# Two residual sums as identity products on TensorE, in a four-layer image kernel

## The chip, the core and the metric

The kernel runs on one core of a Trainium2 chip. The metric is the device time of one execution in microseconds (us). The kernel before was run three times: 5684.69, 5682.38 and 5680.2 us, a median of 5682.38 us.

A core has five engines with a queue of instructions each. PE (TensorE) multiplies matrices and writes only to PSUM, a small memory of eight banks; PEld is its weight load, which runs beside the products. DVE (VectorE), ACT (ScalarE) and POOL (GpSimd) work on tensors; SP only issues DMAs. Each queue is worked off in order, so an instruction that waits holds up all behind it on its engine.

## The reference

The input `x` has 16 images of 64 x 64 tokens (4096) with 256 channels, in float32. Four layers follow one another, each a group norm without scale, a function of it, and a residual sum:

```
x = x + nearest_code(gn(x))        # layer 0: nearest of 1024 code vectors, per token
x = x + attention_rows(gn(x))      # layer 1: sigmoid attention within each row of 64 tokens
x = x + gate(gn(x)) * gn(x)        # layer 2: a scalar gate per token, from a softmax over 4096
x = x + linear_attention(gn(x))    # layer 3: 4 heads of 32, output projection, layer norm over channels
```

In layer 1, `f`, `g` and `h` are projections of the normed input with biases; the scores of a row are `f g^T`, and `sigmoid(scores) h` is added to `x`. In layer 3 the output projection is normed over the channels, multiplied by `gamma`, and `beta` and the residual are added. Two residual sums are what the change touches: that of layer 1 and that of layer 3.

## The kernel before

**Layout.** An image is cut into 8 chunks (`NCHUNK`) of 512 tokens (`CW`). A chunk is mostly held channel-major, as a tile `[128, 2, 512]` of float32: partition is the channel within a half `k` of the 256 channels (`NK` = 2), the free axis is the token. Between stages the chunks go through DRAM (`x1_d`, `x2_d`, `x3_d`). The input is given twice, as tokens (`x`) and channel-major (`xT`); the output is written as tokens.

**Stages, per image.** `stats0` takes the first norm's statistics. `stage1` (layer 0) finds the codes: distances on PE (L403, 512 columns at a time, into a bank pair `pd`), the maximum on DVE (L409, L414), a gather by POOL (L415), transposes back to channel-major (L378, copied out by ACT at L381). `layer1` is described below. `rows2` and `stage2` (layer 2) form three rows per image and then 64 pairs of an exponential on ACT (L645) and a weighted sum on DVE (L648), each over 128 x 2048. `gate2` applies the gate (L702 on ACT, L703 on DVE). `stage3` (layer 3) makes a pass over the chunks for keys, queries and values (L765, L782), and then an output pass.

**Order.** Lines 932 to 968 plan the images: each stage of each image is a task with a start and a length in units of one image, and a heap merges the steps of all generators by their due times. So five or six stages of different images are interleaved in the queues of all engines. The order within each queue is fixed before the run; blocks marked `high_priority` are put ahead. In the middle of the run the pattern repeats for each image.

**PSUM.** `bank(...)` gives one bank of 512 float32 per partition, of four (`ps_m`). `wide(...)` gives a pair of banks, 1024 float32, of two (`ps_w`); the pairs are shared by `pd` (layer 0's distances), `ph` (layer 1's values) and `po` (layer 1's result).

**Layer 1's chunk.** `attend` projects the chunk `xt` (L482, L493), copies the values out (L502, ACT, 128 x 1024), forms the scores (L513) and the attention weights (L518, L522). `mix` multiplies: 8 products of 128 x 128 into the pair `po` (L533), DVE adds `po` to the chunk in place (L538, 128 x 1024), DVE takes the next norm's statistics of it (`bn_stats`, L266), and SP stores the chunk one step later (L545) and loads the chunk after next.

**Layer 3's output.** The chunk `xt` (L892 loads it again) is channel-major and the output is wanted as tokens, so for each pair of 128-token blocks PE transposes the residual into a bank (4 transposes of 128 x 128, L902), adds the projection with the query block as weights (2 products with 256 columns, L908) and adds a row vector over the channels by a product of a block of ones with `x_row` (L912, bfloat16). ACT copies the bank to `y` (L913), and SP writes 4 blocks of 128 tokens at a time (L923, L926), 256 channels of a token being contiguous.

`x_row` holds `xm_` = `beta` minus a mean, a vector over the channels. `put_row` (L145 to 158) makes it once per image, in the first chunk of the key pass (L789): `xm_` is copied on ACT, 8 idle bfloat16 products (`busy`, L135) run, the vector is turned by `by_identity` (L176), and it is split into three bfloat16 parts by two rounds of an ACT cast (L156) and a small product (L157), and a last cast (L158).

Two further lines serve the prediction as rows: L597, an ACT copy of a bank with a bias vector, and L381, an ACT copy after which DVE takes `bn_stats` of the copied chunk.

Of the kernel before, what the change touches and what calls it, by code (L numbers as in the profile page):

```python
# [16 lines left out]
P = 128  # L17
C = 256
# [25 lines left out]
def kernel(  # L44
# [25 lines left out]
    def bank(name):  # L70
        return ps_m.tile([P, 512], F32, tag="pm", name=name)
# [55 lines left out]
    def row_tile(name):  # L127
        t = const.tile([P, C], BF16, name=name)
        nc.gpsimd.memset(t, 0.0)
        return t  # L130
# [6 lines left out]
                skip_group_check=True,  # L137
            )

    h_row, qv_row, x_row = row_tile("h_row"), row_tile("qv_row"), row_tile("x_row")  # L140

    def twice(row):
        return row.unsqueeze(1).to_broadcast([P, 2, C])

    def put_row(dst, v, weight, tag, plus=None, idle=0):  # L145

        v3 = small.tile([P, NK, PARTS], F32, tag="v3", name=f"v3_{tag}")
        nc.scalar.copy(v3, v.unsqueeze(2).to_broadcast([P, NK, PARTS]))
        pb = bank(f"prow_{tag}")
        busy(pb, idle)  # L150
        row = pb[:PARTS, :C]
        weight(row, v3, plus)

        for n in range(PARTS - 1):
            top = small.tile([PARTS, C], BF16, tag="ptop", name=f"top_{tag}_{n}", bufs=1)
            nc.scalar.copy(top, row)  # L156
            nc.tensor.matmul(row, lhsT=below[:, n, :], rhs=top, start=False, stop=True, skip_group_check=True)  # L157
        nc.scalar.copy(dst[0:PARTS, :], row)  # L158

    def by_weight(w):  # L160
# [9 lines left out]
                    skip_group_check=True,  # L170
                )
        return make

    def by_identity(out, v3, plus):
        for k in range(NK):
            nc.tensor.matmul(  # L176
                out[:, k * P : (k + 1) * P], lhsT=v3[:, k, :], rhs=ident, start=(k == 0), stop=(k == NK - 1),
                skip_group_check=True,
            )


    e_raw = s2p.tile([P, NK, CODES], F32, tag="x0b", name="e_raw", bufs=2)
# [258 lines left out]
    def layer1(b):  # L441
# [84 lines left out]
        def mix(ch):  # L526

            at, h = ats.pop(ch), hs.pop(ch)
            po = wide(f"po_{tag}_{ch}")
            for k in range(NK):  # L530
                for t in range(CH):
                    m = (k * CH + t) * P
                    nc.tensor.matmul(  # L533
                        po[:, m : m + P], lhsT=h[:, t, k * P : (k + 1) * P], rhs=at[:, t, :, :].rearrange("p r i -> p (r i)"),
                        start=True, stop=True,
                    )
            X = xt[ch].rearrange("p k n -> p (k n)")
            nc.vector.tensor_tensor(X, po, X, ALU.add)  # L538
            chunk_stats(st2, xt[ch], ch)
            if ch + 2 < NCHUNK:  # L540
                load(ch + 2)
# [174 lines left out]

    def stage3(b):
        tag = f"s3_{b}"
        dst = out[b].rearrange("(t p) c -> p t c", p=P)
        x3 = x3_d.pop(b)  # L720
        scale, nmean, xm_ = norm3.pop(b)
        wk_n = wts.tile([P, NK, P], F32, tag="wk_n", name=f"wk_{tag}")
# [35 lines left out]
        for ch in range(NCHUNK):  # L758
            xt = xb.tile([P, NK, CW], F32, tag="xb", name=f"xk_{tag}_{ch}")
            nc.sync.dma_start(out=xt, in_=x3[ch])  # L760
            if ch > 0:
                normalize(ch - 1)
            pk = bank(f"pk_{tag}_{ch}")
            for k in range(NK):
                nc.tensor.matmul(pk, lhsT=wk_n[:, k, :], rhs=xt[:, k, :], start=(k == 0), stop=(k == NK - 1))  # L765

            now = nkm[:, ch : ch + 1]
            nc.vector.tensor_reduce(now, pk, AX.X, ALU.max, negate=True)
            if ch > 0:
                last = nkm[:, ch - 1 : ch]  # L770
                nc.vector.tensor_scalar(now, now, last, None, ALU.min)
                nc.scalar.activation(al[:, ch : ch + 1], last, AF.Exp, scale=-1.0, bias=now)
            kx = s3p.tile([P, CW], F32, tag="v2", name=f"kx_{tag}_{ch}", bufs=7)
            nc.scalar.activation(kx, pk, AF.Exp, bias=now, accum_out=ks[:, ch : ch + 1])
            qv = s3p.tile([P, CH, 2, P], F32, tag="u4", name=f"qv_{tag}_{ch}")
            qvs[ch] = qv
            for pr in range(CH // 2):
                pqv = bank(f"pqv_{tag}_{ch}_{pr}").rearrange("p (j n) -> p j n", j=2)
                for j in range(2):
                    t = 2 * pr + j  # L780
                    for k in range(NK):
                        nc.tensor.matmul(  # L782
                            pqv[:, j, :], lhsT=xt[:, k, t * P : (t + 1) * P], rhs=wqv_n[:, k, :],
                            start=(j == 0 and k == 0), stop=False, skip_group_check=True,
                        )
                nc.tensor.matmul(pqv, lhsT=ones3, rhs=twice(qv_row), start=False, stop=True, skip_group_check=True)
                nc.scalar.copy(qv[:, 2 * pr : 2 * pr + 2, :, :].rearrange("p j s n -> p j (s n)"), pqv)
            if ch == 0:
                put_row(x_row, xm_, by_identity, f"x_{tag}", idle=8)  # L789
            yield 5  # L790
            pkt = bank(f"pkt_{tag}_{ch}")
            for t in range(CH):
                nc.tensor.transpose(pkt[:, t * P : (t + 1) * P], kx[:, t * P : (t + 1) * P], ident)
            ek = s3p.tile([P, CH, P], F32, tag="v2", name=f"ek_{tag}_{ch}", bufs=7)
            nc.scalar.copy(ek.rearrange("p t d -> p (t d)"), pkt)
            if ch > 0:
                queries(ch - 1)

            q4 = qv[:, :, 0, :].rearrange("p t (h d) -> p t h d", d=DH)
            qm = small.tile([P, CH, HEADS], F32, tag="qm", name=f"qm_{tag}_{ch}")  # L800
            nc.vector.tensor_reduce(qm, q4, AX.X, ALU.max)  # L801
            nc.gpsimd.tensor_tensor(q4, q4, qm.unsqueeze(3).to_broadcast([P, CH, HEADS, DH]), ALU.subtract)  # L802
            nc.scalar.activation(qv[:, :, 0, :], qv[:, :, 0, :], AF.Exp)

            pc = bank(f"pc_{tag}_{ch}")
            for t in range(CH):
                nc.tensor.matmul(pc[:, :P], lhsT=ek[:, t, :], rhs=qv[:, t, 1, :], start=(t == 0), stop=(t == CH - 1))
            if ch > 0:
                nc.vector.scalar_tensor_tensor(
                    ctxa, ctxa, al[:, ch : ch + 1], pc[:, :P], op0=ALU.mult, op1=ALU.add  # L810
                )
            else:
                nc.vector.tensor_copy(ctxa, pc[:, :P])
            yield 5
# [75 lines left out]
        for ch in range(NCHUNK):  # L890
            xt = xb.tile([P, NK, CW], F32, tag="xb", name=f"xo_{tag}_{ch}")
            nc.sync.dma_start(out=xt, in_=x3[ch])  # L892
            qT = qs[ch]
            y = s3p.tile([P, CH, C], F32, tag="u4", name=f"y_{tag}_{ch}")
            for pr in range(2):
                if pr == 1 and ch + 1 < NCHUNK:
                    deviate(ch + 1)
                px = bank(f"pxo_{tag}_{ch}_{pr}").rearrange("p (j c) -> p j c", c=C)
                for j in range(2):
                    t = 2 * pr + j  # L900
                    for k in range(NK):
                        nc.tensor.matmul(  # L902
                            px[:, j, k * P : (k + 1) * P], lhsT=xt[:, k, t * P : (t + 1) * P], rhs=ident,
                            is_transpose=True, start=(j == 0 and k == 0), stop=False, skip_group_check=True,
                        )
                for j in range(2):
                    t = 2 * pr + j
                    nc.tensor.matmul(  # L908
                        px[:, j, :], lhsT=qT[:, t * P : (t + 1) * P], rhs=wctx[:, 1, :], start=False, stop=False,
                        skip_group_check=True,  # L910
                    )
                nc.tensor.matmul(px, lhsT=ones3, rhs=twice(x_row), start=False, stop=True, skip_group_check=True)  # L912
                nc.scalar.copy(y[:, 2 * pr : 2 * pr + 2, :], px)  # L913
                if pr == 0:
                    if ch + 2 < NCHUNK:
                        form(ch + 2)
                    if ch + 3 < NCHUNK:
                        fetch(ch + 3)
                else:
                    if ch + 2 < NCHUNK:  # L920
                        variance(ch + 2)
                    if before is not None:
                        nc.sync.dma_start(out=dst[:, (ch - 1) * CH : ch * CH, :], in_=before)  # L923
                yield 3
            before = y
        nc.sync.dma_start(out=dst[:, TOK // P - CH :, :], in_=before)  # L926

# [75 lines left out]
```

## Time and profile before

| | |
|---|---|
| median of three runs | 5682.38 us |
| the profiled execution | 5674.06 us |
| its span, first to last instruction | 5672.1 us |
| mean granted TensorE clock | 0.962 |
| DMA: moved, mean rate | 1059.26 MB, 187 GB/s |
| busiest DMA queue, share of 16 engines | 46.5% |

The profile is of one execution. Its page gives busy time and share for each engine, the chain of work that ended last, and groups of instructions: line, engine, operation, what is written from what, shape, count, busy time in total, mean of one in ns, and the idle time just before with what ended it. A float32 matrix product stands in the trace as two instructions, a transpose as one, a bfloat16 product as one. Matmuls are pipelined: a group's mean is one instruction's time from start to end, and the distance from start to start of the next, which the timeline shows, is what it takes from PE. The granted clock is the share of full speed that TensorE got in a stretch.

### The profile page before, as it was taken

How to read it: one execution, taken by the hardware profiler on the slowest of the kernel's cores; microseconds unless marked ns; L12 is line 12 of the kernel's file. 1: busy time of each engine (PE TensorE's matmuls, PEld its weight loads, DVE VectorE, ACT ScalarE, POOL GpSimd, SP SyncE). 2: the span in 40 equal slices, each digit the busy share in tenths (PEclk: the TensorE clock that was granted, in tenths of full speed). 3: DMA queues.
4: the chain of work that ended last, by engine and by line, in shares of the span. 5: the costliest groups of instructions: out<-in, count | busy, mean ns of one | idle time of the engine just before them, and what ended most of it. 6: DMA issues, size and time to landing. Idle time of an engine off the chain costs nothing.

```text
span 5672.1 us, 76096 instructions
## 1 busy us (share of the span) xinstructions
PE 5162.0 (91%) x26927; PEld 3189.6 (56%) x26927; DVE 5049.3 (89%) x7186; ACT 4571.1 (81%) x6642; POOL 1801.5 (32%) x1076
## 2 busy tenths in 40 slices
PE   7977889989999999999999999999999999987788
PEld 3534446545656566565655656565565656564556
DVE  7589799899999999999999999999999999988882
ACT  4468589888989898888978888898888879887873
POOL 2223234323333333334333333333333333321221
PEclk9988999999999999999999999999999999998889
DMA  8553744655665757566575656657575675745543
GB/s 254 174 178 84 232 115 144 214 163 185 196 198 175 224 159 236 171 211 198 185 234 155 216 185 200 210 173 236 160 224 183 201 219 156 222 149 176 200 157 119
DMA packets 521365, 1059.26 MB, mean 187 GB/s; under 512 B 52504, under 2 KB 266392, under 8 KB 512792
## 3 DMA queue, kind: packets, MB, share of 16 engines
q1 hardware_dynamic: 406288, 885.11, 46.5%
q0 software_dynamic: 73728, 67.14, 8.3%
q10 hardware_dynamic: 40968, 102.13, 4.6%
q8 instruction: 214, 3.51, 0.3%
q14 instruction: 167, 1.37, 0.1%
HBM read 751.18 MB, written 303.04 MB: 186 GB/s over the span
## 4 chain that ended last, share of the span: by engine, by line
PE 46%; DVE 17%; ACT 16%; issue 6%; DMA 5%; POOL 4%; SPq 0%; ACTq 0%; DVEq 0%; POOLq 0%
PE pd_s L403 14%; ACT ex_s L645 7%; DVE ex_s L648 7%; PE ph_l L493 4%; PE pxo_s L908 3%; PE pqv_s L782 3%; PE po_l L533 2%; PE pk_s L765 2%; ACT nn_s L398 2%; POOL qv_s L802 2%; PE pz_s L857 2%; DVE i_s L414 2%; DVE nn_s L409 2%; PE pxo_s L902 2%; PE pvr_s L865 2%
## 5 line engine op out<-in xcount | busy, mean ns | idle before, releaser
L648 DVE CUSTOM_DVE_ANT_0 ex_s<-ex_s,x2b 128x2048 f32<-128x2048 f32 x1024 | 2360.4, 2312 | 77.6 <-ACT ex_s L645 74.6
L645 ACT ACTIVATE ex_s<-x0b,nmax_s,x_r 128x2048 f32<-128x2048 f32 x1024 | 2138.6, 2089 | 40.7 <-DVE num_s L648 30.5
L403 PE MATMUL pd_s<-e,xn_s 128*128 128x512 f32 x4096 | 1971.1, 614 | 43.9 <-DVE m L409 27.9
L415 POOL DMA_INDIRECT xc_s<-in_emb_rows,i_s x512 | 1113.7, 2175 | 1852.7 <-DVE i_s L414 1337.5
L403 PEld LDWEIGHTS pd_s<-e,xn_s 128*128 128x128 f32 x4096 | 745.8, 195 | 778.8 <-issue 669.1
L409 DVE CUSTOM_DVE_ANT_0 nn_s<-pd_s,nn_s 128x1024 f32<-128x1024 f32 x512 | 619.9, 1212 | 113.5 <-PE pd_s L403 63.0
L414 DVE FIND_INDEX8 i_s<-m,nn_s 128x8 uint32<-128x1024 f32 x512 | 622.9, 1217 | 0.0
L398 ACT ACTIVATE nn_s<-ne,nx_s 128x1024 f32<-128x1024 f32 x512 | 582.5, 1143 | 33.1 <-DVE nx_s L369 18.7
L493 PE MATMUL ph_l<-wh_l,xt_l 128*128 128x256 f32 x2048 | 519.6, 390 | 28.7 <-DVE m L409 16.9
L782 PE MATMUL pqv_s<-wqv_s,xk_s 128*128 128x256 f32 x2048 | 489.3, 381 | 0.0
L493 PEld LDWEIGHTS ph_l<-wh_l,xt_l 128*128 128x128 f32 x2048 | 379.7, 192 | 138.9 <-issue 69.0
L782 PEld LDWEIGHTS pqv_s<-wqv_s,xk_s 128*128 128x128 f32 x2048 | 389.1, 191 | 120.6 <-issue 59.7
L802 POOL TENSOR_TENSOR qv_s<-qv_s,qm_s 128x512 f32<-128x512 f32 x128 | 221.6, 1731 | 662.6 <-DVE qm_s L801 363.2
L868 POOL TENSOR_TENSOR lrs_s<-lrs_s,mhalf 128x4 f32<-128x4 f32 x128 | 178.0, 1391 | 677.2 <-ACT lrs_s L867 663.3
L756 POOL TENSOR_TENSOR qv_s<-qv_s,qd_s 128x512 f32<-128x512 f32 x128 | 214.4, 1675 | 249.0 <-DVE qd_s L755 132.0
L533 PE MATMUL po_l<-blk,h_l 128*128 128x128 f32 x2048 | 282.1, 288 | 3.0 <-DVE m L409 1.5
L533 PEld LDWEIGHTS po_l<-blk,h_l 128*128 128x128 f32 x2048 | 260.6, 200 | 41.1 <-issue 24.5
L908 PE MATMUL pxo_s<-wctx_s,qo_s 128*128 128x256 f32 x1024 | 269.2, 386 | 2.2 <-DVE qo_s L876 2.2
L765 PE MATMUL pk_s<-xk_s,wk_s 128*128 128x512 f32 x512 | 256.0, 620 | 1.0 <-DMA xk_s<-x_g 0.9
L913 ACT COPY y_s<-pxo_s 128x512 f32<-128x512 f32 x256 | 147.5, 580 | 132.4 <-PE pxo_s L912 116.0
L378 PE MATMUL pt_s<-ident,xc_s 128*128 128x128 f32 x1024 | 156.7, 282 | 105.2 <-DMA xc_s<-in_emb_rows,i_s 79.0
L351 ACT ACTIVATE sq_s<-xt_s,first 128x512 f32<-128x512 f32 x256 | 200.2, 806 | 37.2 <-DMA x0b<-rows_r 21.0
(206 smaller groups left out, 7322.0 us busy)
## 6 DMA issues: line engine op xcount, KB each, us to landing
xs_s<-in_xT SPq DMA_DIRECT2D x128, 512.0 KB
xt_s<-in_xT SPq DMA_DIRECT2D x128, 512.0 KB
xc_s<-in_x SPq DMA_DIRECT2D x128, 512.0 KB
x_s<-xt_s ACTq DMA_DIRECT2D x128, 512.0 KB
xt_l<-x_s SPq DMA_DIRECT2D x128, 512.0 KB
x_l<-xt_l SPq DMA_DIRECT2D x128, 512.0 KB
xr_r<-x_l SPq DMA_DIRECT2D x128, 512.0 KB
xg_g<-x_l SPq DMA_DIRECT2D x128, 512.0 KB
```

Of the source, the lines that this page charges most:

```text
L398: nc.scalar.activation(nn, ne2, AF.Identity, bias=nx2[ch][:, t : t + 1])
L403: nc.tensor.matmul(pd[:, cols], lhsT=xn[ch][:, k, t * P : (t + 1) * P], rhs=e2[:, k, cols], start=(k == 0), stop=(k == NK - 1),)
L409: nc.vector.tensor_tensor_reduce(out=nn, in0=pd, in1=nn, scale=1.0, scalar=-3.0e38, op0=ALU.add, op1=ALU.max, accum_out=m8[:, 0:1],)
L414: nc.vector.max_index(i8, m8, nn)
L415: nc.gpsimd.indirect_dma_start(out=xc[ch][:, t, :], out_offset=None, in_=emb_rows, in_offset=bass.IndirectOffsetOnAxis(ap=i8[:, 0:1], axis=0),
L493: nc.tensor.matmul(ph[:, t, :], lhsT=X[:, k, t * P : (t + 1) * P], rhs=wh_n[:, k, :], start=(t % 2 == 0 and k == 0), stop=False, skip_grou ...
L533: nc.tensor.matmul(po[:, m : m + P], lhsT=h[:, t, k * P : (k + 1) * P], rhs=at[:, t, :, :].rearrange("p r i -> p (r i)"), start=True, stop ...
L645: nc.scalar.activation(ex, x0b, AF.Exp, bias=nmax[:, T : T + 1], scale=x01[:, T, 1:2], accum_out=den[:, h, T : T + 1])
L648: nc.vector.tensor_tensor_reduce(out=ex, in0=ex, in1=x2b, scale=1.0, scalar=0.0, op0=ALU.mult, op1=ALU.add, accum_out=num[:, h, T : T + 1],)
L765: nc.tensor.matmul(pk, lhsT=wk_n[:, k, :], rhs=xt[:, k, :], start=(k == 0), stop=(k == NK - 1))
L782: nc.tensor.matmul(pqv[:, j, :], lhsT=xt[:, k, t * P : (t + 1) * P], rhs=wqv_n[:, k, :], start=(j == 0 and k == 0), stop=False, skip_group ...
L908: nc.tensor.matmul(px[:, j, :], lhsT=qT[:, t * P : (t + 1) * P], rhs=wctx[:, 1, :], start=False, stop=False, skip_group_check=True,)
```

## The change

**Layer 1.** The residual comes in on PE: for each half `k`, a float32 product with `ident` as weights and the 512 columns of the chunk opens the bank, and the 4 products of L533 accumulate on it. DVE's sum is gone; ACT copies the pair of banks (128 x 1024) back into the chunk. The statistics stay on DVE.

**Layer 3.** The output is left channel-major. For each half `pr` of the channels, a float32 product of `ident` with the chunk's 512 columns opens a bank, and one product with a 128 x 128 block of the projection as weights and the 512 queries closes it. ACT's copy becomes an ACTIVATE that adds `xm_` as a bias vector, one value per partition. The transposes, the products with 256 columns, the product with `x_row`, and all that made `x_row` are gone. The DMA to the output writes 128 partitions with 4 KB contiguous each. The host reorders axes of the result.

```diff
-    h_row, qv_row, x_row = row_tile("h_row"), row_tile("qv_row"), row_tile("x_row")
+    h_row, qv_row = row_tile("h_row"), row_tile("qv_row")
...
-    def by_identity(out, v3, plus):
-        for k in range(NK):
-            nc.tensor.matmul(
-                out[:, k * P : (k + 1) * P], lhsT=v3[:, k, :], rhs=ident, start=(k == 0), stop=(k == NK - 1),
-                skip_group_check=True,
-            )
...
             po = wide(f"po_{tag}_{ch}")
             for k in range(NK):
+                nc.tensor.matmul(
+                    po[:, k * CW : (k + 1) * CW], lhsT=ident, rhs=xt[ch][:, k, :], start=True, stop=False,
+                    skip_group_check=True,
+                )
                 for t in range(CH):
                     m = (k * CH + t) * P
                     nc.tensor.matmul(
                         po[:, m : m + P], lhsT=h[:, t, k * P : (k + 1) * P], rhs=at[:, t, :, :].rearrange("p r i -> p (r i)"),
-                        start=True, stop=True,
+                        start=False, stop=(t == CH - 1), skip_group_check=True,
                     )
-            X = xt[ch].rearrange("p k n -> p (k n)")
-            nc.vector.tensor_tensor(X, po, X, ALU.add)
+            nc.scalar.copy(xt[ch].rearrange("p k n -> p (k n)"), po)
             chunk_stats(st2, xt[ch], ch)
...
-        dst = out[b].rearrange("(t p) c -> p t c", p=P)
+        dst = out[b].rearrange("c p (k n) -> c p k n", k=NK)
...
-            if ch == 0:
-                put_row(x_row, xm_, by_identity, f"x_{tag}", idle=8)
...
-            y = s3p.tile([P, CH, C], F32, tag="u4", name=f"y_{tag}_{ch}")
-            for pr in range(2):
+            y = s3p.tile([P, NK, CW], F32, tag="u4", name=f"y_{tag}_{ch}")
+            for pr in range(NK):
                 if pr == 1 and ch + 1 < NCHUNK:
                     deviate(ch + 1)
-                px = bank(f"pxo_{tag}_{ch}_{pr}").rearrange("p (j c) -> p j c", c=C)
-                for j in range(2):
-                    t = 2 * pr + j
-                    for k in range(NK):
-                        nc.tensor.matmul(
-                            px[:, j, k * P : (k + 1) * P], lhsT=xt[:, k, t * P : (t + 1) * P], rhs=ident,
-                            is_transpose=True, start=(j == 0 and k == 0), stop=False, skip_group_check=True,
-                        )
-                for j in range(2):
-                    t = 2 * pr + j
-                    nc.tensor.matmul(
-                        px[:, j, :], lhsT=qT[:, t * P : (t + 1) * P], rhs=wctx[:, 1, :], start=False, stop=False,
-                        skip_group_check=True,
-                    )
-                nc.tensor.matmul(px, lhsT=ones3, rhs=twice(x_row), start=False, stop=True, skip_group_check=True)
-                nc.scalar.copy(y[:, 2 * pr : 2 * pr + 2, :], px)
+                px = bank(f"pxo_{tag}_{ch}_{pr}")
+                nc.tensor.matmul(px, lhsT=ident, rhs=xt[:, pr, :], start=True, stop=False)
+                nc.tensor.matmul(px, lhsT=wctx[:, 1, pr * P : (pr + 1) * P], rhs=qT, start=False, stop=True)
+                nc.scalar.activation(y[:, pr, :], px, AF.Identity, bias=xm_[:, pr : pr + 1])
...
-                        nc.sync.dma_start(out=dst[:, (ch - 1) * CH : ch * CH, :], in_=before)
+                        nc.sync.dma_start(out=dst[ch - 1], in_=before)
...
-        nc.sync.dma_start(out=dst[:, TOK // P - CH :, :], in_=before)
+        nc.sync.dma_start(out=dst[NCHUNK - 1], in_=before)
...
-    o = nc.dram_tensor("out_0", (x.shape[0], TOK, C), F32, kind="ExternalOutput").ap()
+    o = nc.dram_tensor("out_0", (x.shape[0], NCHUNK, P, NK * CW), F32, kind="ExternalOutput").ap()
...
-    return r.results[0]["out_0"].reshape(x.shape)
+    y = r.results[0]["out_0"].reshape(x.shape[0], NCHUNK, P, NK, CW)
+    return y.transpose(0, 1, 4, 3, 2).reshape(x.shape)
```

## The prediction

> **What bounds the kernel now.** I read the page's engine line and its chain of the work that ended last first, since the change moves work from DVE to PE and ACT.
>
> ```profile
> PE 5162.0 (91%) x26927; PEld 3189.6 (56%) x26927; DVE 5049.3 (89%) x7186; ACT 4571.1 (81%) x6642; POOL 1801.5 (32%) x1076
> PE 46%; DVE 17%; ACT 16%; issue 6%; DMA 5%; POOL 4%; SPq 0%; ACTq 0%; DVEq 0%; POOLq 0%
> ```
>
> PE and DVE are equally busy, but the chain stands on PE for 46% of the span and on DVE for 17%. Busy shares are a mean over unlike stages, so I looked for the stretches. PE's wait for POOL's L756 recurs in the timeline at 2633.09 and at 2967.58 us: one image takes 334.5 us. I cut one image where the chain of waits changes its colour and asked for busy times of each engine in these five stretches (columns: stretch, length, busy us and instructions of PE, PEld, DVE, ACT, POOL, then the granted clock, DMA share, GB/s).
>
> ```profile
> 2633.00:2668.00 35.00, 33.92 (x165) 20.94 (x166) 31.71 (x52) 27.25 (x46) 13.62 (x11) 0.95 0.61 194
> 2668.00:2783.00 115.00, 107.02 (x578) 68.00 (x577) 106.31 (x151) 104.15 (x148) 39.46 (x20) 0.99 0.50 152
> 2783.00:2892.00 109.00, 105.93 (x641) 72.39 (x640) 102.12 (x140) 90.06 (x129) 32.80 (x18) 0.98 0.69 219
> 2892.00:2931.00 39.00, 33.69 (x165) 16.95 (x163) 38.29 (x52) 32.09 (x49) 15.75 (x11) 1.00 0.74 230
> 2931.00:2968.00 37.00, 34.22 (x146) 19.13 (x143) 34.39 (x56) 31.17 (x44) 15.10 (x7) 1.00 0.72 246
> ```
>
> I call them E, A, B, C and D. In B, a third of the image, PE is busy 97%, and the pieces of the chain there add up to 99.5 us on PE, 0.5 on ACT and none on DVE. Four pieces of it:
>
> ```profile
> 2823.07 0.86 PE pz_s L857 x2
> 2823.93 0.86 PE pd_s L403 x2
> 2824.79 0.86 PE pxo_s L908 x4
> 2827.12 1.98 PE po_l L533 x16
> ```
>
> Both edits sit here: by the same windows for single lines, B holds 64 of L533's 128 instructions per image (4 of 8 chunks of layer 1) and 56 of L908's 64 (7 of 8 chunks of layer 3's output). In A the chain is mixed: ACT 46.8 us, PE 33.0, DVE 17.9, POOL 8.5. In C it is 12.0 on DVE and 10.0 on PE; in D 14.2 on PE, 9.1 on DMA, 9.2 on DVE.
>
> **Prices on PE.** The PE timeline gives them from start to start:
>
> ```profile
> 2829.37 0.60 PE L902 MATMUL pxo_s<-ident,xo_s 128*128 128x128 f32 x4
> 2829.81 1.03 PE L908 MATMUL pxo_s<-wctx_s,qo_s 128*128 128x256 f32 x4
> 2830.67 0.38 PE L912 MATMUL pxo_s<-x_row,ones 128*128 128x512 bf16 x1
> 2830.89 0.95 PE L865 MATMUL pvr_s<-one,qz_s 128*128 128x1 f32 x8
> ...
> 2832.17 3.60 PE L403 MATMUL pd_s<-e,xn_s 128*128 128x512 f32 x8
> 2835.61 1.02 PE L857 MATMUL pz_s<-qo_s,gram_s 128*128 128x512 f32 x2
> ```
>
> Eight instructions of L403 are four float32 products with 512 columns: 2835.61 - 2832.17 = 3.44, so 0.86 us each. Half a chunk of layer 3's output costs 0.44 + 0.86 + 0.22 = 1.52 us.
>
> **Layer 1, per chunk.** PE gains two identity products, 2 x 0.86 = 1.72 us; 128 chunks make 220 us. An identity product that isn't a transpose has no cheaper row: L176, with `ident` as one operand, runs as two instructions too. DVE loses the add and ACT gains a copy of the same size out of a bank pair, for which L502 is the row:
>
> ```profile
> L538 DVE TENSOR_TENSOR xt_l<-po_l,xt_l 128x1024 f32<-128x1024 f32 x128 | 155.1, 1212 | 14.5 <-PE po_l L533 14.3
> L502 ACT COPY h_l<-ph_l 128x1024 f32<-128x1024 f32 x128 | 129.6, 1013 | 67.2 <-PE ph_l L498 64.9
> L913 ACT COPY y_s<-pxo_s 128x512 f32<-128x512 f32 x256 | 147.5, 580 | 132.4 <-PE pxo_s L912 116.0 <-issue 12.6 <-DMA out<-y_s 1.0
> L597 ACT ACTIVATE rows_r<-pr_r,brow_r 128x512 f32<-128x512 f32 x32 | 21.8, 682 | 55.3 <-PE pr_r L593 55.3
> ```
>
> So DVE -155 us and ACT +130 us. The first identity product waits for nothing new: its chunk is already read by L482 and L493, and the pair `po` has to be free as before. New is that DVE's `bn_stats` waits for ACT. Behind it on DVE stand L409, which frees a pair for PE, and L648. The same pattern exists at L381: there DVE waited 22.6 us in all for 256 statistics. And the copy stands on ACT in front of exponentials (2.09 us each) for which L648 waits; before, the add stood on DVE in the same way. A pair now comes free through ACT: PE waited 5.2 us for L502 at L403, a few us for L538. I take these waits as zero, with 0 to +23 us for the range; below zero is possible where DVE's own queue was the late one, at most the 14.5 us in L538's row.
>
> **Layer 3, per chunk.** Before 2 x 1.52 = 3.04 us of PE, after 4 products of 0.86 = 3.44: +0.40, times 128 is +51 us. ACT's copy gets a bias vector: L597 against L913, +0.10 us x 256 = +26 us; ACT has room in B (90 of 109, none of the chain). The output DMA keeps its place on SP; its issue takes 0.39 us against 0.32 for the channel-major store L545, and SP is nowhere on the chain, so zero, with the last DMA's few us as the most that could be won.
>
> **`x_row`, per image.** Gone are 8 idle products, L176 and two small products, 1.73 + 0.53 + 0.20 + 0.20 = 2.66 us in D's chain, 16 images 43 us of PE; ACT loses 3.1 + 11.2 + 5.7 = 20 us, off the path. Next late there is L756 on POOL (PE waits for it at 2967.58, 2 us idle), so the gain lies between 0 and 2.66; I take all, since the chain runs over these pieces and through L409 to that wait.
>
> **Sum.** PE +220 + 51 - 43 = +228 us, DVE -155, ACT +136. How much of it reaches the end differs by stretch; I weigh each engine's change by its share of the chain there over its busy time.
> - B: PE 4 x 1.72 + 7 x 0.40 = 9.7, times 99.5/105.9: +9.1. DVE and ACT: nothing on the chain; if PE's cover went, DVE would give back 3 adds, 3.6 us.
> - A: 3 chunks. PE 5.2 x 33/107 = +1.6; ACT 3.0 x 46.8/104 = +1.4; DVE -3.6 x 17.9/106 = -0.6. Together +2.4.
> - C: PE +0.6, ACT +0.4, DVE 2 adds -2.4 x 12/38 = -0.8: +0.2.
> - D: -2.7.
>
> That is +9.0 us per image of 334.5. The first image and the last two have no such B; there I take a third. 13 x 9.0 + 3 x 3.0 = +126 us. The whole span's shares are a second way: PE 228 x 0.46 x 5672/5162 = +115, DVE -155 x 0.17 x 5672/5049 = -30, ACT 136 x 0.16 x 5672/4571 = +27: +112. I take +118: 5674 + 118 = 5792 for an execution like the profiled one. That one lies 8 us under the median of the runs, so the forecast is **5800 us**, 2.1% slower.
>
> [...]
>
> **Rivals.**
> - *PE is the bound everywhere.* For it: PE is busy 94% in mid-run and the same wait always comes back to it. Then all 228 us at the clock of 0.98 count: 5682 + 233 = 5915. Against: in A the chain has 47 us on ACT and 18 on DVE, and PE has 8 us idle there.
> - *The idle time takes it up.* PE has 20.2 us idle in the cut image (335 less 314.8) and needs 228/16 = 14.3 more. With DVE's 9.7 us gone, PE's waits for DVE shrink: 5682. Against: the idle time lies in A, C and D, the load in B.
> - *Faster, because DVE sets the pace.* For it: DVE is busy 38.3 of 39 us in C, and 93% over the image. PE would have to come down to 1% idle: 314.3 us per period of 334.5 and 14.3 more, over 0.99, are 331.9 us, 2.6 less, 16 images -42: 5640. It decides from the point where PE's idle share falls under 1.8% (328.6 of 334.5); B, the densest stretch, still has 2.8%.
> - *The identity product is cheaper than an ordinary one* (one instruction as in a transpose, 0.43 us): PE +220 becomes +110 and +51 becomes -59, in all +8, DVE's -30 then decides, about 5675. L176 speaks against it.
>
> **Chances.** The forecast, between 5735 and 5880, has 0.68; PE as the bound everywhere 0.11; taken up 0.08; faster by DVE 0.11; cheaper product 0.02. A difference of under 0.2% is about what a measurement of this kernel can't tell from none. Faster by more 0.12, within 0.2% 0.08, slower by more 0.80. The range goes from the taken-up case to the edge of the forecast's own plus part of the first rival: 5680 to 5890. The unknown waits (-14 to +23) and the lost gain in D (+43) lie inside it.
>
> **What would show it.** L538 gone, a copy of about 1.01 us in its place; L533's line with two more float32 products of 0.86 us per chunk; layer 3's half chunk at 1.72 instead of 1.52 us; PE's busy time near 5390, DVE's near 4895, ACT's near 4705; the image's period at 342 to 344 us, the growth in the stretch where layer 3's output and layer 1 overlap; the chain with more PE and less DVE. Wrong if the period stays at 334 with PE over 98% busy, if the identity product starts its successor after 0.43 us, or if DVE's waits for ACT at L266 grow past 23 us.

## The result, and the profile after

The changed kernel takes 5724.57 us (median of four runs, 5719.19 to 5737.11), the kernel before 5681.29 us in four runs beside it: a ratio of 1.0079, interval 1.0061 to 1.0097. It is slower by 43 us, where 118 had been forecast: the right sign, and a third of the size. The profiled execution took 5722.29 us, its span is 5720.6 us, the mean granted clock 0.970.

The engine line and the chain of the changed kernel's page:

```profile
PE 5361.2 (94%) x25935; PEld 3125.8 (55%) x25935; DVE 4922.3 (86%) x7058; ACT 4689.3 (82%) x6706; POOL 1791.9 (31%) x1075
PE 63%; DVE 11%; ACT 9%; DMA 4%; issue 4%; POOL 3%; ACTq 0%; SPq 0%; POOLq 0%; DVEq 0%
```

PE is busy 199 us longer, but the span grew by 48.5. So PE's idle time fell from 510 to 359 us: three quarters of the added work went into it. In the groups (busy in total, mean ns of one, idle time before) the new operations have their expected prices. The line numbers of the changed kernel are lower by up to 20: L396 is the old L403, L644 the old L648, L530 the old L533.

```profile
L524 PE MATMUL po_l<-xt_l,ident 128*128 128x512 f32 x512 | 270.1, 609 | 1.5 <-DVE m L402 1.5
L534 ACT COPY xt_l<-po_l 128x1024 f32<-128x1024 f32 x128 | 128.7, 1006 | 52.2 <-PE po_l L530 51.5
L259 DVE BATCH_NORM_STATS2 st_l<-xt_l 128x6 f32<-128x512 f32 x256 | 163.9, 680 | 39.8 <-ACT xt_l L534 38.9
```

So has the new half chunk of layer 3, here in PE's timeline (start, duration): from start to start 0.86 us for the identity product and 0.86 for the projection, 1.72 in all.

```profile
2862.46 1.02 PE L893 MATMUL pxo_s<-xo_s,ident 128*128 128x512 f32 x2
2863.32 1.02 PE L894 MATMUL pxo_s<-qo_s,wctx_s 128*128 128x512 f32 x2
2864.18 1.02 PE L851 MATMUL pz_s<-qo_s,gram_s 128*128 128x512 f32 x2
```

Where the time came from shows in the starts of one instruction of each image, the product that brings the bias into layer 1's row (`prow_h_l<-ident,bh`), in both timelines. The table gives its start in us for some images and, in the last two columns, the mean distance of an image to the next (images are counted from 0):

| | image 1 | image 4 | image 8 | image 15 | end | images 4 to 6 | images 8 to 14 |
|---|---|---|---|---|---|---|---|
| before | 499.8 | 1353.1 | 2663.7 | 4999.6 | 5672.1 | 325.7 | 333.7 |
| after | 511.2 | 1377.5 | 2715.7 | 5055.0 | 5720.6 | 334.1 | 334.2 |
| difference | +11.4 | +24.4 | +52.0 | +55.4 | +48.5 | +8.4 | +0.5 |

**The loss lies in the first half of the images; the later half as a whole lost next to nothing.** What sets them apart: in the steady part of the run, images 6 to 13 also carry the input statistics of a later image on DVE, 16 operations of 680 ns each, 10.9 us per image. The row of the kernel before:

```profile
L266 DVE BATCH_NORM_STATS2 st_s<-xs_s 128x6 f32<-128x512 f32 x256 | 167.1, 680 | 12.3 <-DMA xs_s<-in_xT 12.0
```

The same starts tell it image by image. Before the change images 4 and 5, without these statistics, take 322.4 and 325.2 us, and images 7 to 13, with them, 332.1 to 339.0. After it, images 4 and 5 take 333.5 and 333.7 us, and images 7 to 13 take 333.6 to 335.9. So the change costs 11.1 and 8.5 us in images 4 and 5, and gains 0.8 in the mean of images 8 to 13. Image 14, which is late but carries no such statistics, pays 8.1 us again; it is the last but one and has some 13 us less on PE than the others, so it counts for less. (Image 6, in the table's column of early images, carries them already.)

One late image cut at the same three instructions in both kernels (products of `prow_h`, `pgr` and `prow_qv`; I call the stretches A, B and D; columns as in the prediction). Before:

```profile
2664.00:2782.00 118.00, 109.10 (x587) 68.57 (x585) 109.28 (x158) 106.61 (x153) 42.26 (x22) 0.99 0.49 147
2782.00:2924.00 142.00, 133.62 (x780) 88.02 (x779) 134.41 (x183) 117.56 (x169) 44.68 (x27) 0.99 0.69 219
2924.00:2998.00 74.00, 71.15 (x319) 40.10 (x317) 68.12 (x107) 60.05 (x94) 29.24 (x18) 0.98 0.72 235
```

After:

```profile
2716.00:2828.00 112.00, 110.74 (x594) 68.92 (x592) 108.12 (x157) 103.44 (x153) 36.19 (x22) 1.00 0.59 171
2828.00:2978.00 150.00, 149.34 (x737) 85.78 (x737) 141.36 (x189) 137.71 (x189) 50.01 (x30) 1.00 0.65 200
2978.00:3051.00 73.00, 68.08 (x292) 38.40 (x290) 55.52 (x94) 50.47 (x79) 26.56 (x17) 0.95 0.70 233
```

B grew by 8 us, as forecast, and A shrank by 6, which had not been. PE's idle time fell from 20.1 us to 6.8. DVE has 7 us more in B and 12.6 less in D though its work fell: the planner, which lays the queues by the steps' costs, laid another order. Counted in DVE's queue (cut where DVE scales the weights `wh` and `wqv`, L308, and at L834), the 64 pairs of exponentials of an image lie 22, 22 and 20 in A, B and D before, and 22, 27 and 15 after. In an earlier image the picture is simpler. Three images of each, before and after:

```profile
1353.00:2330.00 977.00, 937.42 (x5025) 583.55 (x5023) 922.91 (x1300) 852.06 (x1237) 339.97 (x195) 0.99 0.63 194
```

```profile
1377.00:2380.00 1003.00, 980.60 (x4837) 574.62 (x4835) 901.24 (x1277) 876.91 (x1249) 333.84 (x194) 0.99 0.61 189
```

PE goes from 96.0% to 97.8%; of 43 us more products (14 per image), 26 show in the time, and 17 found idle time here too. DVE, at 922.91 of 977 us, was busy 94.5% in these early images before the change, no less than in the late ones (93.4%). So it isn't shown that PE alone set their pace then.

### The profile page after: what moved, and what is told of

It is laid out like the page before. It is cut to its first block, busy times and chain, and to the rows that moved or that the text cites. A ratio compares the mean times of both kernels' runs of the same rounds, so it can differ in the third digit from the quotient of the medians.

```text
span 5720.6 us, 74037 instructions
## 1 busy us (share of the span) xinstructions
PE 5361.2 (94%) x25935; PEld 3125.8 (55%) x25935; DVE 4922.3 (86%) x7058; ACT 4689.3 (82%) x6706; POOL 1791.9 (31%) x1075
## 4 chain that ended last, share of the span: by engine, by line
PE 63%; DVE 11%; ACT 9%; DMA 4%; issue 4%; POOL 3%; ACTq 0%; SPq 0%; POOLq 0%; DVEq 0%
PE pd_s L396 21%; PE ph_l L486 6%; DVE ex_s L644 5%; PE pxo_s L893 4%; ACT ex_s L641 4%; PE pxo_s L894 4%; PE po_l L524 3%; PE po_l L530 3%; PE pqv_s L778 3%; PE pk_s L761 2%; PE pz_s L851 2%; DMA xc_s<-in_emb_rows,i_s 2%; PE pr_r L589 2%; PE pvr_s L859 2%; DVE i_s L407 2%
## 5 line engine op out<-in xcount | busy, mean ns | idle before, releaser
L644 DVE CUSTOM_DVE_ANT_0 ex_s<-ex_s,x2b 128x2048 f32<-128x2048 f32 x1024 | 2363.0, 2318 | 127.3 <-ACT ex_s L641 126.9
L396 PE MATMUL pd_s<-e,xn_s 128*128 128x512 f32 x4096 | 1960.7, 613 | 23.9 <-DVE m L402 16.1
L408 POOL DMA_INDIRECT xc_s<-in_emb_rows,i_s x512 | 1096.8, 2142 | 1996.1 <-DVE i_s L407 1594.8
L396 PEld LDWEIGHTS pd_s<-e,xn_s 128*128 128x128 f32 x4096 | 748.5, 195 | 786.4 <-issue 713.8
L486 PE MATMUL ph_l<-wh_l,xt_l 128*128 128x256 f32 x2048 | 507.7, 386 | 0.9 <-DVE m L402 0.9
L862 POOL TENSOR_TENSOR lrs_s<-lrs_s,mhalf 128x4 f32<-128x4 f32 x128 | 220.5, 1723 | 585.7 <-ACT lrs_s L861 565.2
L530 PEld LDWEIGHTS po_l<-blk,h_l 128*128 128x128 f32 x2048 | 271.0, 192 | 113.8 <-issue 111.6
L530 PE MATMUL po_l<-blk,h_l 128*128 128x128 f32 x2048 | 277.3, 276 | 0.0
L752 POOL TENSOR_TENSOR qv_s<-qv_s,qd_s 128x512 f32<-128x512 f32 x128 | 198.2, 1548 | 244.6 <-DVE qd_s L751 120.1
L893 PE MATMUL pxo_s<-xo_s,ident 128*128 128x512 f32 x512 | 272.7, 615 | 0.0
L524 PE MATMUL po_l<-xt_l,ident 128*128 128x512 f32 x512 | 270.1, 609 | 1.5 <-DVE m L402 1.5
L894 PE MATMUL pxo_s<-qo_s,wctx_s 128*128 128x512 f32 x512 | 267.1, 603 | 0.7 <-DVE qo_s L870 0.7
L895 ACT ACTIVATE y_s<-pxo_s,xm_g 128x512 f32<-128x512 f32 x256 | 174.3, 681 | 101.9 <-PE pxo_s L894 99.3
```

The lines of the kernel that those rows point to most:

```text
L396: nc.tensor.matmul(pd[:, cols], lhsT=xn[ch][:, k, t * P : (t + 1) * P], rhs=e2[:, k, cols], start=(k == 0), stop=(k == NK - 1),)
L408: nc.gpsimd.indirect_dma_start(out=xc[ch][:, t, :], out_offset=None, in_=emb_rows, in_offset=bass.IndirectOffsetOnAxis(ap=i8[:, 0:1], axis=0),
L486: nc.tensor.matmul(ph[:, t, :], lhsT=X[:, k, t * P : (t + 1) * P], rhs=wh_n[:, k, :], start=(t % 2 == 0 and k == 0), stop=False, skip_grou ...
L530: nc.tensor.matmul(po[:, m : m + P], lhsT=h[:, t, k * P : (k + 1) * P], rhs=at[:, t, :, :].rearrange("p r i -> p (r i)"), start=False, sto ...
L644: nc.vector.tensor_tensor_reduce(out=ex, in0=ex, in1=x2b, scale=1.0, scalar=0.0, op0=ALU.mult, op1=ALU.add, accum_out=num[:, h, T : T + 1],)
L893: nc.tensor.matmul(px, lhsT=ident, rhs=xt[:, pr, :], start=True, stop=False)
```

## The experiments

Theories: **the limits** (DVE's work sets the late images' pace before the change, PE's work the early ones', and PE's everywhere after it, so that a product costs nothing where DVE's add goes with it, and its time where PE was the limit); **the order** (waits that the queue order makes set the period, and each edit shuffles them); and, against both, **the prediction's even price** of 9 us in each image. All ratios are to the kernel before on the same chip, with their intervals; the last two columns are the mean distance of an image to the next in the profiled execution, which for layer 3 alone was the longest of four (5748.37 us), so that its distances are somewhat high.

| run | time, us | ratio | images 4 to 6 | images 8 to 14 |
|---|---|---|---|---|
| kernel before | 5675 to 5681 | 1 | 325.7 | 333.7 |
| changed kernel | 5724.57 | 1.0079 [1.0061, 1.0097] | 334.1 | 334.2 |
| layer 1 alone | 5738.84 | 1.0107 [1.0088, 1.0125] | 331.7 | 335.8 |
| layer 3 alone | 5726.23 | 1.0081 [1.0063, 1.0099] | 331.1 | 338.7 |
| products without use | 5705.93 | 1.0050 [1.0033, 1.0068] | 332.1 | 332.9 |
| copy without products | 5662.43 | 0.9975 [0.9961, 0.9989] | 335.0 | 329.2 |
| order held | 5803.50 | 1.0215 [1.0183, 1.0247] | 336.8 | 340.7 |
| before, fewer statistics | 5611.75 | 0.9880 [0.9854, 0.9906] | 326.2 | 325.6 |
| after, fewer statistics | 5714.22 | 1.0061 [1.0042, 1.0080] | 333.5 | 333.7 |
| layer 3 with its row | 5699.24 | 1.0026 [1.0011, 1.0042] | 328.6 | 334.1 |
| layer 1, late images | 5667.21 | 0.9983 [0.9966, 1.0000] | 326.2 | 333.1 |
| layer 1, early images | 5715.72 | 1.0068 [1.0041, 1.0096] | 331.5 | 333.1 |
| layer 1, late, half | 5657.40 | 0.9969 [0.9952, 0.9986] | 325.7 | 330.4 |
| after, with the row | 5770.28 | 1.0169 [1.0152, 1.0186] | 338.2 | 335.7 |

**The two edits by themselves.** Layer 1's edit alone, with layer 3 as before:

> Layer 1's edit alone; layer 3 and x_row as before. The busiest engine sets the period: PE needs 315 + 13.8 = 329 us per image, and at 98% busy that is 335 to 337 us, all images alike: about 5735 us, nearly the whole loss of the change. The forecast's theory (each stretch by its share of the chain): about +7 us per image, 5785 us.

Layer 3's edit alone, without `x_row`, with layer 1 as before:

> Layer 3's edit and the end of x_row alone; layer 1's add stays on DVE. Both theories: PE +3.2 and -2.7 us per image, DVE unchanged, so within 0.2% of before, 5670 to 5690 us. If the transposes or the row vector cost more than their rows say, under 5670.

The first came out at +63 us, near the lower figure, but not in all images alike (+6.0 us in the early ones, +2.1 in the late). The second, +51 us, was expected by neither theory. The two sum to +114, yet both together cost 43: the parts don't add, which no sum over single operations can give. What stands out in the layer-3 run is a wait in PE's list from 2700 to 4700 us (in total, times, longest) that takes 2.2 us in the kernel before:

```profile
PE pg_n L278 <- DVE mv_n L274: 20.9, 11, 4.4
```

**PE's load without DVE's relief, and the reverse.** The kernel before, in which each chunk's pair is first written by the identity products and then overwritten, so that DVE's add stays:

```diff
             for k in range(NK):
+                nc.tensor.matmul(
+                    po[:, k * CW : (k + 1) * CW], lhsT=ident, rhs=xt[ch][:, k, :], start=True, stop=True,
+                    skip_group_check=True,
+                )
                 for t in range(CH):
```

> The kernel before with two identity products more per chunk of layer 1, whose result is thrown away: the next products clear the bank. PE +220 us, DVE and ACT unchanged. If PE's idle time takes the products up whatever DVE does: about as layer 1's edit alone, 5735 us. If DVE's relief paid for most of them: 5780 us or more.

And the kernel before with ACT's copy in place of DVE's add and no products; layer 1's residual is left out of the computation:

```diff
-            X = xt[ch].rearrange("p k n -> p (k n)")
-            nc.vector.tensor_tensor(X, po, X, ALU.add)
+            nc.scalar.copy(xt[ch].rearrange("p k n -> p (k n)"), po)
```

> The kernel before with layer 1's residual left out: ACT copies the bank pair into the chunk, DVE adds nothing, PE has no products more. DVE -155, ACT +130, PE unchanged. If DVE set the pace in the images that also take statistics of a later image (periods of 334 to 339 us): 5 to 9 us less in each of them, 5615 to 5645 us. If PE set the pace throughout: within 0.2% of before.

163 us more of PE cost only 30, less than any theory said: 6 us in an early image, nothing in a late one. DVE's relief gained 13 us, less than expected, since it gained 4 to 5 us in a late image and lost 9 in an early one. The early loss isn't PE's work, which is as before; PE's list of waits from 1375 to 2380 us, three images, begins with one that the kernel before hasn't among its first:

```profile
PE pgt_s L665 <- DVE gate_s L662: 19.5, 3, 6.8
```

This is a wait of another order, and the first sign that both theories hold a part.

**The order by itself.** The changed kernel, in which the last 14 exponential pairs of an image's second row may not stand ahead of the last query scale of the image before in DVE's queue. No operation is added. The pairs then lie 21, 22 and 21 over the three stretches: nearly as before the change (22, 22 and 20), but with one more in D.

```diff
+            mark = [i for i in nc.cur_bb.bb.instructions if i.engine == sums[0, 0, 0].ins.engine][-1]
+            for T in range(18, NT):
+                if (b + 1, 1, T) in sums and b + 1 < nb - 1:
+                    tc.add_manual_dep(
+                        sums[b + 1, 1, T].ins, mark.name,
+                        mybir.DependencyInfo(mybir.DependencyClass.NoSync, mybir.DependencyReason.DATA), reason="hold",
+                    )
```

> The changed kernel with one thing added: the exponential sums (b+1,1,18) to (b+1,1,31) may not stand ahead of image b's query scale in VectorE's queue, so that a late image's pairs of exponentials lie 22/22/21 over the three stretches as in the kernel before, and not 22/27/15. No operation is added or taken away. Theory 1 (the planner paid for the identity products by moving five pairs into the dense stretch; the order carries the gain): the late images' period goes from 335 us to 341 to 342, 10 of them, and the time to 5780 to 5800 us, a ratio of 1.018 to 1.021. Theory 2 (the idle time of TensorE takes up the products whatever the order): 5715 to 5735 us, 1.007 to 1.010, period 334 to 336.

It came out at 1.0215, a period of 340.7: the order carries 6 us per late image. The same three stretches, to be laid beside those of the changed kernel:

```profile
2730.10:2843.10 113.00, 111.63 (x601) 70.17 (x600) 104.44 (x153) 104.66 (x151) 42.65 (x21) 1.00 0.55 168
2843.10:2987.10 144.00, 142.93 (x706) 80.91 (x704) 125.63 (x174) 124.49 (x175) 42.51 (x27) 0.99 0.63 198
2987.10:3071.70 84.60, 74.10 (x317) 41.01 (x318) 73.41 (x113) 62.95 (x94) 30.85 (x19) 0.96 0.68 220
```

PE is busy 328.7 us as against 328.2: the work is the same. Its idle time is 12.9 instead of 6.8. B is 6 us shorter and D 11.6 longer. In D's timeline, one image later, PE stands idle for the statistics that DVE makes behind two exponential sums:

```profile
3394.13 1.88 PE L396 MATMUL pd_s<-e,xn_s 128*128 128x512 f32 x4
3400.03 0.56 PE L278 MATMUL pg_n<-mv_n,dmat 128*128 128x2 f32 x2 [4.02 <-DVE mv_n L274]
...
3403.04 1.91 PE L396 MATMUL pd_s<-e,xn_s 128*128 128x512 f32 x2
```

The wait is that of the layer-3 run. In the changed kernel the same `pg_n` starts without one. From 2700 to 4700 us it takes 22.9 us in six waits here, 3.8 per image, so that with the slower clock behind such a wait (0.50 behind one of them, last section) it may make up most of the 6 us.

One count fits this wait in every profile. The two runs that hold 21 pairs in D, this one and layer 3 alone, have it (22.9 and 20.9 us); all other kernels hold 15 to 20 there and have 0 to 2.9 us of it, or 8.2 without layer 1's residual. So the 6 us may be the price of that one pair more, and not of the five that the changed kernel had moved; this run doesn't separate the two.

**DVE's work by itself, before and after.** For the eight images from the ninth on, DVE copies 8 columns of a chunk in place of the input's statistics, and those images are normed with the figures of an earlier image. This edit in the kernel before:

```diff
-            chunk_stats(st, xt, ch)
+            if b <= EARLY:
+                chunk_stats(st, xt, ch)
+            else:
+                nc.vector.tensor_copy(seen, xt[:, 0, 0:8])
...
+        if b > EARLY:
+            norm0[b] = tuple(first[:, b - EARLY - 1, n, :] for n in range(3))
+            return
```

> The kernel before with the statistics of the input left out for the images past the first eight (VectorE copies 8 columns of a chunk in place of four bn_stats, and those images are normed by the figures of an image that was read earlier), which takes some 10.9 us of VectorE's 314 off a late image. Theory 1 (VectorE's 314 us of 335 set the pace of the late images before the change): period 324 to 328, some 60 to 80 us less, 5600 to 5620 us, a ratio of 0.987 to 0.990. Theory 2 (waits between the engines in their order set it, no engine alone): period 331 to 335, 5640 to 5680 us, 0.994 to 1.000.

The same edit in the changed kernel:

> The changed kernel with the same statistics left out. Theory 1 (TensorE sets the pace now, and VectorE has time to spare): period stays at 333 to 335, 5705 to 5725 us, a ratio of 1.005 to 1.009. Theory 2 (waits between the engines set it, VectorE still among them): period 328 to 331, 5655 to 5685 us, 0.997 to 1.002.

Their engine lines, in this order:

```profile
PE 5127.8 (91%) x26839; PEld 3165.9 (56%) x26839; DVE 4988.4 (89%) x7106; ACT 4566.7 (81%) x6618; POOL 1799.4 (32%) x1060
```

```profile
PE 5347.7 (93%) x25847; PEld 3110.4 (54%) x25847; DVE 4884.8 (85%) x6978; ACT 4687.8 (82%) x6682; POOL 1777.6 (31%) x1059
```

Before, 61 us less of DVE took 70 us off the time. (The statistics left out are the 10.9 us per image of the expectation, though two per chunk and not four; the small copies put in their place took 3.4 back.) But the edit also leaves out 11 small instructions per image on PE, those that finish the norm, and PE was busy 34 us less. So each microsecond of DVE was worth a little over one (70/61) if PE's part counted for nothing, as the limits theory has it, and 0.6 if it counted in full. The copy without products gave less: in a late image 4.5 us for 9.3 of DVE, 0.5 for each. After, 38 us less of DVE and 13.5 less of PE took off some 10, and the intervals of the two ratios overlap. The same instructions went in both kernels, so the difference between 70 and 10 isn't PE's small products: the limit of the late images has changed its engine. Both times and both periods lie in the bands of the limits theory.

**Layer 3 with its row.** Layer 3's edit alone, with `put_row(x_row, ...)` kept at its place and read by nothing:

> The edit of layer 3 alone, with the row of the residual's mean still built at the first chunk of the key pass (its eight idle products and six small ones too) and used by nothing. Against the run of the layer-3 edit alone (1.008), theory 1 (what cost time there was that this row's products no longer stand in a stretch where TensorE waits, and the products behind them run at the lower clock or late): 5675 to 5690 us, a ratio of 1.000 to 1.003. Theory 2 (the last pass in its new form costs it, by 51 us of products and 400 of ScalarE's copies at another shape): 5725 to 5755 us, 1.008 to 1.014.

1.0026 for 1.0081: with 14 instructions *more* on PE per image (43 us in all by the forecast's prices) this kernel is faster. The ratio is in the first theory's band, the time 9 us above it. The wait for `mv_n` is back at 2.2 us. Without the row's steps the planner had put 21 pairs in D and 21 in A, with them 20 and 22: one pair less ahead of the statistics that PE waits for.

**Where layer 1's products cost.** Layer 1's edit, for some images and chunks alone, layer 3 as before. The condition is `b >= EARLY` (from the eighth image), `b < EARLY` (the first seven), and `b >= EARLY and ch % 2 == 0`:

```diff
+            onpe = b >= EARLY
             for k in range(NK):
+                if onpe:
+                    nc.tensor.matmul(
+                        po[:, k * CW : (k + 1) * CW], lhsT=ident, rhs=xt[ch][:, k, :], start=True, stop=False,
...
+            if onpe:
+                nc.scalar.copy(X, po)
+            else:
+                nc.vector.tensor_tensor(X, po, X, ALU.add)
```

> Layer 1's edit alone and only in the images from the eighth on, whose stretches carry the statistics of a later input on VectorE; the first seven keep the add of VectorE. Theory 1 (two limits: VectorE sets the pace of the late images before the change and TensorE of the early ones, so the products cost some 10 us in each early image and nothing in a late one): 5665 to 5700 us, a ratio of 0.998 to 1.004, late period 333 to 337. Theory 2 (each image pays about the same, 8 to 9 us, as the prediction had it): 5735 to 5760 us, 1.010 to 1.014.

> Layer 1's edit alone and only in the first seven images. Theory 1 (two limits): the whole loss of the layer-1 edit alone (1.0107) is here: 5725 to 5755 us, a ratio of 1.008 to 1.013, with the periods of the fourth to eighth image 331 to 336 and the late ones as before. Theory 2 (each image pays about the same): about half of it, 5700 to 5715 us, 1.004 to 1.006.

> Layer 1's edit alone, in the images from the eighth on, and there in the chunks 0, 2, 4 and 6 only: a late image has 8.5 us more on TensorE (315 to 324) and 6 less on VectorE (314 to 308). Theory 1 (two limits): both engines stay under 97 % of a shorter period, 327 to 331 us: 5610 to 5660 us, a ratio of 0.988 to 0.996. Theory 2 (each image pays for its products): 5705 to 5720 us, 1.004 to 1.007. Theory 3 (the order that the planner lays sets the period, by several us either way): no number; anything beyond 1.002 or between the two would speak for it.

In the late images the edit costs nothing: 93 us more of PE, 79 less of DVE, and 12 us off the time, at the edge of what can be told from none. In the early ones it costs 36 us of the whole edit's 63 (1.0068 of 1.0107). That is between the two theories' bands, and its interval, 1.0041 to 1.0096, reaches into both: the mark of image 8 stands 53 us later than before, and the late images give some of it back, while with the edit in all images they lose 15 us more. The even price fails in the first run; the second can't decide. The half edit has the lowest time of the versions that compute the reference (0.9969), ahead of both kernels; its interval overlaps with that of the late images alone. It lies at the weak edge of what the limits would give: its period is 330.4 where 327 to 331 was expected, its time 5657 us where 5610 to 5660 was, its ratio just above 0.988 to 0.996.

The third theory keeps a part here too: a late image has the same instructions in the run of layer 1 alone and in that of the late images alone, and its period, over the five images 9 to 13, is 336.7 in the one and 330.3 in the other.

**The row beside both edits.** The changed kernel, with the row built again and read by nothing:

> The changed kernel with the row of the residual's mean built again at the first chunk of the key pass (eight idle products and the small ones, some 43 us of TensorE in all, 2.7 per image) and used by nothing. Theory 1 (TensorE sets the pace of the changed kernel in every image, so each product more is paid): 5745 to 5770 us, a ratio of 1.012 to 1.017. Theory 2 (the row's products help by themselves, as they did beside the layer-3 edit alone, 1.0026 with the row for 1.0081 without): 5690 to 5710 us, 1.002 to 1.006.

```profile
PE 5394.7 (94%) x26159; PEld 3129.3 (54%) x26159; DVE 4935.7 (86%) x7058; ACT 4704.5 (82%) x6770; POOL 1773.5 (31%) x1076
```

33 us more of PE's busy time made it some 46 us slower (51 by the ratios, 40 by the profiled spans). The same steps that helped beside the layer-3 edit alone are paid in full here, 20 us by image 8 and 11 more in the next seven. After the change, PE's microseconds are the ones that count. That 33 us cost more than themselves isn't explained; the order may have its part in it.

## Why the prediction was right in sign and wrong in size

**The prices held.** An identity product took 0.86 us, the copy out of the bank pair 1.006 us (from L502: 1.013), the copy with a bias 681 ns (from L597: 682), layer 3's half chunk 1.72 us. Busy time changed by +199 us on PE (forecast +228), -127 on DVE (-155), +118 on ACT (+136). On PE, a part of the difference is that untouched products ran shorter (L533's mean fell from 288 to 276 ns, at a mean clock of 0.970 for 0.962).

**The step that failed is the sum: "That is +9.0 us per image of 334.5", taken 13 times.** It priced a microsecond of each engine by that engine's share of the chain in one late image, and carried the price to all images. Two things are wrong in it.

- *The price of DVE in a late image.* "DVE -3.6 x 17.9/106 = -0.6" in A, and nothing in B. The two runs that took work from DVE before the change put its price in a late image between 0.5 and a little over one, not at 0.2. A share of the chain says what ended last, not what the time would do if that engine had less work: in these late images taking work from DVE shortened the period, though the chain passed mostly through PE and ACT. In the cut of the result, B came out as forecast (+8 for the +9.3 of B and C), D at -1 for -2.7, and A at -6 for +2.4. So the late images paid 0.5 us each for the forecast 9.0.
- *One image for all.* The image cut was a late one. In images 4 to 6, where DVE has less to do, the price was 8.4 us. That it is near the forecast's 9.0 is luck: the forecast worked its figure out for a late image, and here PE went from 96.0% to 97.8% busy.

Of the span's 48.5 us, 11.4 are there by image 1, 40.6 come between images 1 and 8, 3.4 between 8 and 15, and the end gives 6.9 back.

**The rivals.** "The idle time takes it up" is what happened in the late images, and its mechanism is the one named: PE's waits for others shrank, from 20.1 us to 6.8 (20.2 less 14.3 had been worked out). The argument against it, "the idle time lies in A, C and D, the load in B", failed because the change doesn't leave the queue order as it was: five pairs of exponentials moved from D to B, and A became 6 us shorter. That this move is what made the idle time usable isn't shown: where the pairs were held back the period was 6 us longer, but D then held one pair more than before the change, too. "DVE sets the pace" had the mechanism of the late images before the change; that it gained nothing agrees with the rival's own condition, that PE's idle share has to fall under 1.8% for a gain: after the change it is 2.0%. "PE is the bound everywhere" is now true of the kernel after, not of the one before.

**The waits.** DVE's wait for ACT's copy was given 0 to 23 us. It is 38.9, outside that range; 27.9 of it lie in the first 500 us, where the add waited 8.0 before. The mark of image 1 is 11.4 us late, and these 20 us of wait may be a part of that; no run separates it. From 2700 to 4700 us the wait doesn't occur.

**PE's busy share.** In the changed kernel the products are busy 98.0% of a late image, and 33 us more of products cost 46: there the busy share of a late image showed what set its pace. Before the change, at 94% in a late image, it did not: in the late images 93 us of products vanished beside 79 us less of DVE, and the unused products of the third run took no time there either.

**What stays open.** Why one order is better than another by 6 us per image is shown at one wait (`pg_n` for `mv_n`, with 21 pairs in D) and isn't reduced to a rule beyond that. Nor is it shown why the two edits alone cost 114 us and together 43, why late images with the same instructions take 336.7 us in one run and 330.3 in another, or what set the pace of the early images before the change.

## What to carry to other kernels

Price an engine's microsecond by taking a little of its work away and timing that; a share of the chain was no such price here, and neither was a busy share of 94%. Look at a steady pattern in more than one place before multiplying it: here one added task on VectorE went with whether the same edit cost 8 us per image or none. And where a planner lays out the queues, an edit can lay them out anew: another order of the same instructions moved the late period by 6.5 us of 334, nearly what the added work cost an early image.

## What the runs showed of the hardware

Behind two waits of some 4 us on PE the granted clock of a stretch of 3 us was 0.50 and 0.65. In the run with the order held, PE idled 4.02 us before 3400.03; in the stretch from 3401 to 3404 us PE was busy throughout at a granted clock of 0.50:

```profile
3401.00:3404.00 3.00, 3.00 (x13) 2.48 (x13) 3.00 (x4) 0.82 (x3) 2.48 (x2) 0.50 0.56 175
```

The small products `pg_n` took 0.56 us there for a pair that takes 0.28 in the changed kernel, and a distance product 1.91 us for 1.02. In the changed kernel a wait of 4.06 us before 3350.95 was followed by a mean clock of 0.65 from 3351 to 3354. In the run with the order held, two shorter ones, of 1.62 and 1.90 us with four transposes (0.66 us) between them, were also followed by a clock of 0.51 from 3376 to 3379 us: there no single wait was as long as 4 us. So these waits on PE cost more than themselves.
